# Gated cross-attention with a routed expert layer: pieces of the expert-weight sums stored and fetched at the end of a step, loads behind the turned blocks, and rows of the first pairs fetched ahead of weights

## The chip, the cores and the metric

The kernel runs on one core of a Trainium2 chip. The metric is device time in microseconds (us). One profiled execution is shown beside the timed runs; the names of engines are those of the profile: PE (TensorE matmuls), PEld (its weight loads), DVE (VectorE), ACT (ScalarE), POOL (GpSimd), SP (SyncE, which here only issues DMAs). A name such as L527 is a line of the kernel. A DMA that SP issues is a row marked SPq: its duration is the time that SP spends on issuing it, not the transfer.

## The reference, cut to what matters

There are 32 batches of 112 rows of x and 375 rows of context, 256 wide. All is float32.

```
lat  = layer_norm(layernorm(x));  ctx = layer_norm(ctx_1024)
q    = lat @ Wq                                  # 16 heads of 64
k, v = split(concat([ctx, lat]) @ Wkv)           # 487 keys per batch
x    = x + tanh(g_xattn) * (softmax(q k^T / 8) v) @ Wout
xf   = layernorm(x)                              # 3584 tokens
best two of softmax(xf @ gate_w), renormalised   # 8 experts
y_e  = gelu(xf @ w1[e] + b1[e]) @ w2[e] + b2[e]  # 256 -> 1024 -> 256
out  = x + tanh(g_ffn) * (sum over the two best experts of score * y_e)
```

## The kernel before, in words

**Attention in 128 steps.** A step n (LAST = 128 of them) handles one batch and four of its heads. Eight steps make a group of two batches; m = n mod 8. The keys and values of a pair of batches are made by seven block products instead of eight (`seven`), whose sums run on DVE (L433, L437, L447) and GpSimd (L423). In a step the scores of step n+1 are computed (L483), their maxima are taken on DVE (L493), ACT takes exponentials (L502) and scales them (L516), DVE turns 32x32 blocks in place (`turn_blocks`, L521), and SP sends the turned blocks to memory (`send_blocks`, L527: four DMAs of 256 KB from one of the two buffers `exs`) and takes them back in another layout (`take_blocks`, L534: one DMA of 1 MB into `exT`). `attend` (L547) uses `exT` a step or two later.

**Order.** The program is written with a manual schedule: every engine runs its instructions in the order in which the Python code emits them, SP's DMAs among them. A step is emitted as: turn and send of step n, attend, scores and first exponentials of n+1, and then five slots h = 0 to 4. A slot runs PE units (`slots[h] + pe[h]`), at h = 1 also `take_blocks(n)`, then scalings, and then the small parts listed in `dve[h]` (which run on DVE, ACT, GpSimd or SP). The last slot has PE units alone.

**Other DMAs on SP in a step.** Every fourth step (n mod 4 = 0) up to n = 111 loads a later batch (`load`: 487 KB in three DMAs). At m = 6 and 7 a slab of x is loaded (`load_slab`, L573), and at m = 1 and 2 a finished slab is stored (`residual`, L597). All of these but the store are emitted between send and take.

**Pieces.** The expert layer too uses seven products on 256-row pairs, so sums of blocks of w1 and w2 are needed. They are made during attention in 64 pieces, one a step, from n = 44 to n = 107, and stored in memory (`ws`). `piece_in` (L1272 or L1277) fetches 256 KB in two DMAs into the only buffer `piece`; `piece_sums` are four GpSimd additions in place (L1303), two in each of two slots (h = 2 and 3); `piece_out` (L1314 or L1317) stores four DMAs of 64 KB. At the start of step n, behind the send, the piece of the step before is stored and the next one is fetched into the same buffer; then comes the take.

**Experts.** Tokens are scattered by GpSimd to their experts' places in memory (`xg`, L726) as groups of slabs are routed. 256-row pairs are fetched from `xg` (`fetch_rows`, L935). Pair 0 runs during the last steps with plain weights (`weights_ahead`, `turn_rows(0)`, `hidden_plain`, `second_plain`), from LAST-6 on. In step LAST-2 `others` closes the pools of the attention and opens those of the experts, and fetches the weights of pair 1 for its first layer (`fetch_first`, L988, seven blocks) and second layer (`fetch_second`, L1005, six blocks) and the rows of pairs 1 to 3. After the last step come `second_plain`, the last `attend`, and then the loop over pairs. `turn_rows` transposes rows on PE (L1023) and copies them out of PSUM (L1027).

Of the kernel before, what the change touches and what calls it, by code (L numbers as in the profile page):

```python
# [23 lines left out]
def kernel(  # L24
# [20 lines left out]
    nc = tc.nc  # L45
# [23 lines left out]
    AHEAD = 3  # L69
# [20 lines left out]
    def ended(b):  # L90

        return (SB - 1) * (b // SB) + b % SB - 1 if b % SB else None
# [85 lines left out]
    if True:  # L178
# [344 lines left out]
        def send_blocks(n):  # L523


            for a in range(QB):
                nc.sync.dma_start(  # L527
                    turned[n % 2][:, :, a, :].rearrange("k j n -> j k n"),
                    exs[n % 2][a * QW : (a + 1) * QW].rearrange("j k q c h r -> j k (q c h r)"),
                )  # L530
# [397 lines left out]
        def fetch_rows(t):  # L928
            m, i = unit_of(t)
            r = number(m, i, 1, PADS - 2 * P if t < PAIRS else PADS)  # L930
            pool, n = (found["early"], 1) if t == 0 else (found["rows"], AHEAD + 3)
            xs[t] = pool.tile([P, 2, C], F32, tag="xs", name=f"xs_{t}", bufs=n)
            if t < PAIRS:
                rows_ = xg[bass.ds(r, 2 * P), :].rearrange("(b p) c -> p b c", p=P)
                nc.sync.dma_start(xs[t], rows_)  # L935
            else:
                nc.sync.dma_start(xs[t][:, 0, :], xg[bass.ds(r, P), :])
# [29 lines left out]
        def fetch_first(t):  # L967

            e, new = found["e", t] = expert_of(t)
            fetch_biases(t, e, found["weights"], 2, (0,))  # L970
            if t < PAIRS:
                s1_, s2_, s3_, s4_ = (
                    (f"s{n + 1}", ws1[bass.ds(e, 1), n].rearrange("o p f -> p (o f)"))
                    for n in range(4)
                )
                a11, a12, a22 = (
                    (n, half_of_w1(e, k, h)) for n, k, h in (("11", 0, 0), ("12", 1, 0), ("22", 1, 1))
                )
                order_ = (a11, s2_, s3_, s1_, a22, a12, s4_)
            else:  # L980
                if t == PAIRS:
                    new_weights("21", [P, 512], "s3")
                order_ = [
                    (n, half_of_w1(e, k, h))
                    for n, k, h in (("11", 0, 0), ("12", 1, 0), ("21", 0, 1), ("22", 1, 1))
                ]
            for n, src in order_:
                nc.sync.dma_start(wt[n], src, **new)  # L988

        def fetch_second(t):  # L990

            e, new = found.pop(("e", t))
            if t < PAIRS:
                t1_, t2_, t3_, t4_ = (
                    (f"t{n + 1}", ws2[bass.ds(e, 1), n].rearrange("o p c d -> p (o c) d"))
                    for n in range(4)
                )
                b11, b2x = ("b11", half_of_w2(e, 0, 0, P)), ("b2x", half_of_w2(e, 1, 0, D))
                order_ = (b11, b2x, t4_, t1_, t3_, t2_)
            else:  # L1000
                if t == PAIRS:
                    new_weights("b1x", [P, NF // 2, D], "t12")
                order_ = (("b1x", half_of_w2(e, 0, 0, D)), ("b2x", half_of_w2(e, 1, 0, D)))
            for n, src in order_:
                nc.sync.dma_start(wt[n], src, **new)  # L1005
            fetch_biases(t, e, found["weights"], 2, (1,))
# [236 lines left out]
        def others(ends):  # L1243

            ends.close()
            found["weights"] = ctx.enter_context(tc.tile_pool(name="wexp2", bufs=1))
            found["rows"] = ctx.enter_context(tc.tile_pool(name="rows2", bufs=1))
            found["tiles"] = ctx.enter_context(tc.tile_pool(name="tiles", bufs=2))
            for n in ("11", "12", "22", "s1", "s2", "s3", "s4"):
                new_weights(n, [P, 512])  # L1250
            for n in ("b11", "t3", "t4"):
                new_weights(n, [P, NF // 2, P])
            new_weights("b2x", [P, NF // 2, D])
            new_weights("t12", [P, 2, NF // 2, P])
            wt["t1"], wt["t2"] = wt["t12"][:, 0], wt["t12"][:, 1]
            fetch_first(1)
            fetch_second(1)
            for t in range(1, 1 + AHEAD):
                fetch_rows(t)


        pieces = [(l, e, c) for e in range(E) for l in range(2) for c in range(NF // 2)]
# [166 lines left out]
        for n in range(LAST):  # L1429
            turn_blocks(n, 1)  # L1430
            send_blocks(n)
            if n % NG == 0:
                b = n // NG
                if b + 4 < B:
                    load(b + 4)
                if b == 1:
                    fill()
            g, m = divmod(n, 2 * NG)


# [53 lines left out]
                        dve[h].append(ln_now[h])  # L1494

            k = n - 44
            if 0 <= k <= len(pieces):
                if k > 0:
                    piece_out(k - 1)
                if k < len(pieces):  # L1500
                    piece_in(k)
                    for h, part in enumerate(piece_sums(k)):
                        dve[2 + h].append(part)
            if n == 1:
                nc.scalar.activation(tg[:, :2], tg[:, :2], AF.Tanh)
                nc.scalar.mul(tg[:, 2:3], tg[:, 1:2], 0.5)
# [3 lines left out]
            for u in range(2):  # L1510
                i = ended(2 * g - 2 + u) if g > 0 else None
                if m == 6 + u and ended(2 * g + u) is not None:
                    load_slab(ended(2 * g + u))
                if i is None:
                    continue
                if m == 1:
                    pe[2 + 2 * u].append(lambda i=i: project(i))
                if m == 1 + u:
                    dve[3 - 3 * u].append(lambda i=i: residual(i))

                m_ = 3 + 2 * u if nb >= B else 3 + 3 * u
                if m == m_:
                    dve[0].append(lambda i=i: normed(i))
                    pe[3].append(lambda i=i: gate_turn(i))
                if m == m_ + 1:
                    pe[0].append(lambda i=i: gate_scores(i))
                    if group[i][1] == groups[group[i][0]] - 1:

                        r, (hits, ids, ids_out) = route_parts(group[i][0], nc.gpsimd)
                        extra = [[part] for part in r[:9]] + [[]] + [[part] for part in r[9:11]]  # L1530
                        if group[i][0] == 0:

                            at = [(j, e) for j in range(2) for e in range(0, E, 2)]
                            for k in range(len(at) + 1):
                                extra.append([lambda p=p: ids(*p) for p in at[k - 1 : k] if k > 0])
                                extra[-1] += [lambda p=p: hits(*p) for p in at[k : k + 1]]
                            extra.append([ids_out])
                        extra += [[part] for part in r[11:]]
# [8 lines left out]
            if n == LAST - 6:  # L1547
                soon.close()
                found["early"] = ctx.enter_context(tc.tile_pool(name="early", bufs=1, side="right"))
                weights_ahead()  # L1550
            if n == LAST - 5:
                fetch_rows(0)
            if n == LAST - 3:
                pe[4].append(lambda: turn_rows(0))
            if n == LAST - 2:

                pe[0].append(lambda: others(ends))
                for h in range(1, 5):
                    pe[h].append(lambda h=h: hidden_plain(h - 1, h))
            if n == LAST - 1:  # L1560
                for h in range(4):
                    pe[h].append(lambda h=h: hidden_plain(h + 4, h + 5))
                pe[4].append(lambda: turn_rows(1))
# [7 lines left out]
            for h in range(5):  # L1571
                for unit in slots[h] + pe[h]:
                    unit()
                if h == 4:
                    break
                if h == 1:
                    take_blocks(n)
                if more and h in (1, 3):
                    norm(n + 1, h // 2)
                if more and h == 3:  # L1580
                    turn_blocks(n + 1, 0)
                then_ = soon_[:]
                del soon_[:]
                do(then_)
                for part in dve[h]:
                    part()

                if outgoing and (h % 2 == 0 or n > LAST - NG):
                    outgoing.pop(0)()
                if extra:  # L1590
                    do(extra.pop(0))
                if more and h == 0:
                    exps(n + 1, 1)
# [120 lines left out]
```

## Time and profile before

| what | value |
|---|---|
| median of 3 runs | 2096.77 us (2092.31 to 2097.70) |
| profiled execution | 2101.99 us |
| its span, first to last instruction | 2100.2 us |
| mean granted PE clock | 0.977 |
| PE busy | 1972.9 us (94%) |
| POOL busy | 991.4 us (47%) |
| DMA queue of SP (q1) | 414 MB, 65.0% of 16 engines' span |
| steps with pieces, 44 to 107 | 557.9 to 1373.3 us |

How to read it: a group row of the page gives line, engine, operation, output and input, shapes and count, then busy time and the mean of one in ns, and then idle time of the engine before it and what ended that. A row of a timeline gives start, duration, engine, line, what it writes and reads and how many were merged, and in brackets the idle time before it with what ended it. A row of waits gives who waited for whom, us in total, times, and the longest. A row of a stretch gives its bounds and length, busy time of the engines, granted clock, DMA share and GB/s.

### The profile page before, as it was taken

Reading aid. Unit: us, or ns where it says so; the run is one execution under the profiler, and the core shown is the slowest. Engines: PE = TensorE matmul, PEld = TensorE weight load, DVE = VectorE, ACT = ScalarE, POOL = GpSimd, SP = SyncE. Lnnn points to the kernel's source line nnn. Section 1 sums busy time; section 2 is a strip of 40 time slices with the busy share of each in tenths; the row PEclk is TensorE's granted clock in tenths of the full one; section 3 lists DMA queues with packets and bytes.
Section 4 is the critical chain, followed back from the end, with each engine's and each line's share of the span. In section 5 each row is a group of like instructions: output and inputs, shape, how many; then the busy total and the mean of one; then the engine's idle time right before and its main releaser. Section 6 shows DMA issues by size and latency. Waiting matters only on the chain. (4 is left out here: it accounts for less than half of the span.)

```text
span 2100.2 us, 41466 instructions
## 1 busy us (share of the span) xinstructions
PE 1972.9 (94%) x14352; PEld 1509.7 (72%) x14352; DVE 1340.1 (64%) x2418; ACT 1157.2 (55%) x2717; POOL 991.4 (47%) x1467
## 2 busy tenths in 40 slices
PE   8999999999999999999999998999997899799998
PEld 4676767676766666666767666667675799799887
DVE  6777676867676777676766766676764367445211
ACT  5666666666666665666656655666644133334333
POOL 5533343444356455544555545553333367757312
PEclk9999999999999999999999999999997899999999
DMA  7767666767677777776777767785666366599773
GB/s 212 211 201 206 180 189 176 199 171 223 189 221 225 225 239 232 228 225 219 232 221 214 227 210 224 218 247 172 184 201 203 124 190 192 142 324 295 201 204 58
DMA packets 264643, 433.44 MB, mean 206 GB/s; under 512 B 34312, under 2 KB 152656, under 8 KB 248048
## 3 DMA queue, kind: packets, MB, share of 16 engines
q1 hardware_dynamic: 251968, 414.39, 65.0%
q0 software_dynamic: 11328, 15.33, 3.8%
q8 instruction: 115, 1.88, 0.4%
q10 hardware_dynamic: 1136, 1.05, 0.2%
q14 instruction: 96, 0.79, 0.1%
HBM read 301.37 MB, written 172.28 MB: 226 GB/s over the span
## 5 line engine op out<-in xcount | busy, mean ns | idle before, releaser
L502 ACT ACTIVATE ex<-bank,nmx 128x512 f32<-128x512 f32 x512 | 348.3, 689 | 262.9 <-DVE nmx L493 262.9
L516 ACT ACTIVATE ex<-ex,rc 128x512 f32<-128x512 f32 x512 | 342.2, 718 | 252.2 <-DVE rc L513 250.8
L493 DVE TENSOR_REDUCE nmx<-bank 128x2 f32<-128x974 f32 x256 | 286.1, 1157 | 115.0 <-PE bank L483 114.9
L521 DVE STREAM_TRANSPOSE ex<-ex 128x1024 f32<-128x1024 f32 x256 | 314.9, 1230 | 28.0 <-ACT ex L516 25.2
L1303 POOL TENSOR_TENSOR piece<-piece 128x128 f32<-128x128 f32 x256 | 116.6, 456 | 333.6 <-DMA piece<-in_L_ffn_w_dram 320.0
L413 PEld LDWEIGHTS ps_v<-wkv_s,tT 128*128 128x128 f32 x1536 | 191.8, 194 | 94.2 <-DVE kT L447 44.8
L483 PE MATMUL bank<-kT,qTs 64*128 64x487 f32 x1024 | 249.5, 606 | 0.0
L413 PE MATMUL ps_v<-wkv_s,tT 128*128 128x128 f32 x1536 | 204.0, 281 | 23.0 <-DVE kT L447 21.2
L447 DVE TENSOR_TENSOR vv<-ps_v,vv 128x512 f32<-128x512 f32 x192 | 131.6, 686 | 143.1 <-PE ps_v L413 65.8
L547 PE MATMUL ps_o<-exT,vv 128*64 128x112 f32 (+1 forms) x4096 | 213.1, 262 | 0.6 <-DMA exT<-turned 0.6
L547 PEld LDWEIGHTS ps_o<-exT,vv 128*64 128x64 f32 (+1 forms) x4096 | 199.1, 137 | 9.1 <-DMA exT<-turned 0.8
L407 PE MATMUL ps_k<-tT,wkv_s 128*128 128x487 f32 x378 | 183.2, 586 | 22.1 <-DVE vv L447 22.0
L423 POOL TENSOR_TENSOR kT<-tmpk,kT 128x487 f32<-128x487 f32 x63 | 77.0, 1222 | 243.7 <-ACT kT L441 243.7
L413 PEld LDWEIGHTS ps_v<-wkv,kvT 128*128 128x128 f32 x1024 | 129.4, 192 | 72.9 <-issue 65.3
L1073 POOL DMA_INDIRECT out_dram<-y,xs x60 | 93.4, 1557 | 167.5 <-DVE y L1097 96.3
L483 PEld LDWEIGHTS bank<-kT,qTs 64*128 64x128 f32 x1024 | 89.8, 189 | 106.7 <-issue 96.0
L447 DVE TENSOR_TENSOR kT<-ps_k,kT 128x487 f32<-128x487 f32 x189 | 123.6, 657 | 59.9 <-POOL kT L423 29.7
L423 POOL TENSOR_TENSOR vv<-tmpv,vv 128x512 f32<-128x512 f32 x64 | 81.2, 1270 | 129.9 <-ACT vv L441 129.9
L413 PE MATMUL ps_v<-wkv,kvT 128*128 128x128 f32 x1024 | 141.5, 281 | 0.0
L407 PE MATMUL ps_k<-kvT,wkv 128*128 128x487 f32 x252 | 130.5, 599 | 0.0
L334 PE MATMUL ps_q<-kvT,wq_sb 128*128 128x224 f32 x512 | 120.0, 356 | 1.4 <-ACT kvT L322 0.7
L1119 ACT ACTIVATE h<-h,b 128x256 f32<-128x256 f32 x160 | 66.2, 495 | 97.6 <-DVE h L1128 97.0
(296 smaller groups left out, 3700.6 us busy)
## 6 DMA issues: line engine op xcount, KB each, us to landing
turned<-ex SPq DMA_DIRECT2D x512, 256.0 KB
exT<-turned SPq DMA_DIRECT2D x128, 1024.0 KB
w<-in_L_ffn_w_dram SPq DMA_DIRECT2D x132, 256.0 KB
w_s<-ws SPq DMA_DIRECT2D x80, 256.0 KB
w_t<-ws SPq DMA_DIRECT2D x80, 256.0 KB
w_b2x<-in_L_ffn_w_dram SPq DMA_DIRECT2D x38, 512.0 KB
piece<-in_L_ffn_w_dram SPq DMA_DIRECT2D x128, 128.0 KB
ws<-piece SPq DMA_DIRECT2D x256, 64.0 KB
```

The source lines that it names most:

```text
L334: nc.tensor.matmul(ps, lhsT=wq_sb[:, k, i * P : (i + 1) * P], rhs=kvT[g][:, k, :, SC:NK], start=(k == 0), stop=(k == KD - 1),)
L407: nc.tensor.matmul(ps, lhsT=w[:, 0, i * P : (i + 1) * P], rhs=x[:, :NK], start=True, stop=True)
L413: nc.tensor.matmul(ps[:, c, :], lhsT=x[:, c * P : (c + 1) * P], rhs=w[:, 1, i * P : (i + 1) * P], start=True, stop=True,)
L423: nc.gpsimd.tensor_tensor(v[o], v[l], v[r], ALU.add)
L447: nc.vector.tensor_tensor(v[at], product(n, w, x), v[at], ALU.add)
L483: nc.tensor.matmul(ps[:, j, :NK], lhsT=qT[b // 2, i][r, b % 2].rearrange("p a i -> p (a i)"), rhs=kT[b, i][r, :], start=True, stop=True,)
L493: nc.vector.tensor_reduce(nmx[b, i], pss[b, i][:, :, :NK], AX.X, ALU.max, negate=True)
L502: nc.scalar.activation(exs[n % 2][:, :, p, :, j, :], ps[:, j, :].rearrange("p (c k r) -> p k c r", c=NCK, r=QW), AF.Exp, bias=nmx[b, i][:, ...
L516: nc.scalar.mul(t, t, rc[:, j : j + 1])
L521: nc.vector.transpose(t, t)
L547: nc.tensor.matmul(ps[y * DH : (y + 1) * DH, r, x * S : (x + 1) * S].rearrange("p (a i) -> p a i", a=QB), lhsT=vv[j][:m, c, x, r, y * DH : ...
L1303: nc.gpsimd.tensor_tensor(o, l, r, op) for o, l, r, op in ops
```

## The change

- Loads of batches, the padding of `xg` and the slab loads are collected in a list `after` and emitted behind `take_blocks(n)` instead of in front of it.
- Pieces: a step that sums piece k does so in slots h = 1 and 2; at the end of slot h = 3 it stores piece k and fetches piece k+1. The first piece is fetched at the end of step 43. Both lie behind the take of the step and in front of the send of the next.
- Rows of pair 0 are fetched in step LAST-6 instead of LAST-5, in front of the weights of pair 0, and both behind the take. Their turned copy is made on ACT instead of DVE.
- `others` fetches only the rows of pair 1. The first weights of pair 1 are fetched behind the take of LAST-2; its second weights and the rows of pairs 2 and 3 behind the take of LAST-1.

```diff
@@ others @@
-            fetch_first(1)
-            fetch_second(1)
-            for t in range(1, 1 + AHEAD):
-                fetch_rows(t)
+            fetch_rows(1)
@@ the loop over steps @@
             turn_blocks(n, 1)
             send_blocks(n)
+            after = []
             if n % NG == 0:
                 b = n // NG
                 if b + 4 < B:
-                    load(b + 4)
+                    after.append(lambda b=b: load(b + 4))
                 if b == 1:
-                    fill()
+                    after.append(fill)
...
             k = n - 44
-            if 0 <= k <= len(pieces):
-                if k > 0:
-                    piece_out(k - 1)
-                if k < len(pieces):
-                    piece_in(k)
-                    for h, part in enumerate(piece_sums(k)):
-                        dve[2 + h].append(part)
+            if k == -1:
+                dve[3].append(lambda: piece_in(0))
+            if 0 <= k < len(pieces):
+                for h in range(2):
+                    dve[1 + h].append(lambda k=k, h=h: piece_sums(k)[h]())
+                dve[3].append(lambda k=k: piece_out(k))
+                if k + 1 < len(pieces):
+                    dve[3].append(lambda k=k: piece_in(k + 1))
...
-                    load_slab(ended(2 * g + u))
+                    after.append(lambda i=ended(2 * g + u): load_slab(i))
...
-                weights_ahead()
-            if n == LAST - 5:
-                fetch_rows(0)
+                after += [lambda: fetch_rows(0), weights_ahead]
             if n == LAST - 3:
-                pe[4].append(lambda: turn_rows(0))
+                pe[4].append(lambda: turn_rows(0, nc.scalar.copy))
             if n == LAST - 2:
                 pe[0].append(lambda: others(ends))
+                after.append(lambda: fetch_first(1))
...
             if n == LAST - 1:
+                after += [lambda: fetch_second(1)]
+                after += [lambda t=t: fetch_rows(t) for t in range(2, 1 + AHEAD)]
...
                 if h == 1:
                     take_blocks(n)
+                    do(after)
```

## The prediction, on record before the result

> **What bounds the kernel now.** I read the page first, then busy time by stretch, then the waits of SP's queue in the stretch with pieces, then that queue in order of time, then the end of the attention.
>
> ```profile
> PE 1972.9 (94%) x14352; PEld 1509.7 (72%) x14352; DVE 1340.1 (64%) x2418; ACT 1157.2 (55%) x2717; POOL 991.4 (47%) x1467
> ...
> L1303 POOL TENSOR_TENSOR piece<-piece 128x128 f32<-128x128 f32 x256 | 116.6, 456 | 333.6 <-DMA piece<-in_L_ffn_w_dram 320.0
> ```
>
> TensorE sets the pace nearly everywhere. GpSimd loses 320 us waiting for pieces, which looks like the prize. By stretch (length, then PE, PEld, DVE, ACT and POOL busy, PE clock, DMA share, GB/s), eight steps without pieces, eight with, and all 64 steps with pieces (n = 44 to 107):
>
> ```profile
> 240.40:338.00 97.60, 95.84 (x695) 68.49 (x694) 71.16 (x116) 62.23 (x146) 34.93 (x48) 1.00 0.65 189
> 936.60:1038.00 101.40, 96.50 (x687) 68.31 (x686) 70.21 (x116) 62.21 (x145) 48.27 (x79) 0.97 0.73 229
> 557.90:1373.30 815.40, 768.53 (x5509) 548.68 (x5508) 567.42 (x968) 498.12 (x1154) 435.27 (x728) 0.98 0.73 224
> ```
>
> Eight steps take 97.6 us with PE 98% busy (94.2 where only one slab is projected), so 64 would take about 774. With pieces they take 815. **At most 41 us** can be won from the pieces. What is left on SP there:
>
> ```profile
> SPq L527 <- DVE ex L521: 93.9, 46, 7.4
> SPq L1277 <- DMA ws<-piece: 65.4, 38, 3.5
> SPq L1272 <- DMA ws<-piece: 63.6, 39, 3.5
> ```
>
> SP has only 93.9/64 = 1.5 us a step to spare before the sends (L527), and waits 129 us for piece stores to land. So SP's chain of one step is nearly as long as a step. That chain decides the change, and I cost it from three places: a step without pieces (252), one that is sent right behind exT (1023), one on a free queue (1037).
>
> ```profile
> 252.01 2.71 SPq L527 DMA_DIRECT2D turned<-ex  x4
> 257.99 0.34 SPq L534 DMA_DIRECT2D exT<-turned  x1
> ```
>
> ```profile
> 1022.66 0.36 SPq L534 DMA_DIRECT2D exT<-turned  x1
> 1023.44 2.36 SPq L527 DMA_DIRECT2D turned<-ex  x4
> 1025.89 4.32 SPq L1317 DMA_DIRECT2D ws<-piece  x4
> 1033.84 0.82 SPq L1277 DMA_DIRECT2D piece<-in_L_ffn_w_dram  x2
> ...
> 1037.93 2.61 SPq L527 DMA_DIRECT2D turned<-ex  x4
> 1040.64 3.40 SPq L1317 DMA_DIRECT2D ws<-piece  x4
> 1045.42 0.81 SPq L1277 DMA_DIRECT2D piece<-in_L_ffn_w_dram  x2
> ```
>
> From first send to landed blocks (when L534 is let go): 257.99 - 252.01 = 6.0 us. From first send to landed stores (when the fetch is let go): 7.5 us on the free queue, 1.5 behind the blocks; but 10.4 us where exT was issued 0.8 us ahead. So what is issued behind exT waits for exT: this queue works in order.
>
> **The pieces, part by part.** Before, a step's SP order is send n, store k-1, fetch k, take n. The stores go out behind the send and land 1.5 us after the blocks, so the wait for the blocks is hidden under the store, and exT (1 MB) moves while SP waits for DVE. After, it is send n, take n, store k, fetch k+1, send n+1. Two waits that overlapped now stand one behind the other, and exT's transfer comes between.
>
> The chain from one send to the next:
> - send to landed blocks: 6.0 us, and 0.3 since the fetch of 0.9 us earlier still moves in front: 6.3.
> - exT, issued then: the trace's DMA records end its last 8 KB packet 4.4 us after issue in quiet steps, 4.6 with landing. (From the rows: its data hold the queue 2.9 + 0.8 = 3.7 us, plus some 1.2 of start and landing, 4.9. I take the smaller.)
> - the four stores behind it: 1.5. Their issue, 0.45 each, is hidden under exT.
> - the fetch, which needs the same buffer and so waits for the stores: 0.9 with its gap.
>
> Sum **13.3 us** against 12.2 for a mean step without pieces. In one step of four the loads (487 KB), now between take and store, add 1.6, at exT's 1 MB in about 3.4 us. Slab loads (two of eight steps) add 0.4. Eight steps: 8 x 13.3 + 2 x 1.6 + 2 x 0.4 = 110.4 us; 64 steps: 883.
>
> SP's lateness stalls nobody at once. A send's buffer is written again by the exponentials of two steps on; a send at 275.90 had landed at 282.3 and its buffer was wanted at about 287.8, so 5.5 us of lateness are free. It grows by 4 to 5 in each load step and is used up in the first three or four steps. Then ACT waits at L502 for the send's transfers, and scores, copies and PSUM behind it on ACT hold PE. Some 8 us of lateness are left over at the end and cost nothing: 883 - 8 = 875, against 815: **+60 us**. GpSimd doesn't help: a piece lands about 2 us after a send, its four sums take 4 x 0.456 = 1.8 us, and they are done before the stores' turn comes at 6.6; its 320 us of waiting don't vanish. Bounds of a chain: 12.5 us if exT and stores overlap by engine skew (64 steps 824, +9) and 14.0 if the sums come late behind GpSimd's scatters or exT is stretched (920, +105).
>
> Here a rule speaks for the change. The Trainium skill (DMA: Bandwidth & Descriptors, Anatomy of one DMA) has one DMA at about 2.0 us plus bytes over 436 GB/s, fitted on the GpSimd path. By it, as an estimate, a 1 MB send lands in 4.4, exT in 4.4, the stores 0.6 later, and with the fetch the chain is 10.4 us, shorter than a step: SP would never bind, and the 41 us could be won. The rows show 6.0 for the send, and exT no shorter than the rule's; the rows decide.
>
> The moved loads, slab loads and padding outside these 64 steps: SP has room there (the send waits for DVE in every step), so nothing, at most 1 us either way.
>
> **The end of the attention.** Two stalls there come from order on the DMA queue.
>
> ```profile
> 1561.50 0.41 SPq L935 DMA_DIRECT2D xs<-xg  x1
> ```
>
> ```profile
> 1569.96 1.08 POOL L726 DMA_INDIRECT xg<-xr,sloti  x1 [8.42 <-DMA xs<-xg]
> ...
> 1628.47 1.09 PE L1023 MATMUL ps_x<-ident,xs 128*128 128x128 f32 x4 [8.32 <-DMA xs<-xg]
> ```
>
> First: rows of pair 0 are fetched at 1561.5 behind 2 MB of weights and land at 1569.9; the scatter into xg waits 8.4 us, GpSimd's sums of kT behind it are late, DVE waits 8.9 and PE 4.7, with the clock at half from 1575 to 1585. After, the rows follow exT of step LAST-6: issue near 1554.9, landed near 1559.6. The first scatter (1554.2 before) now waits 5 us, hidden: GpSimd's next sums start at 1557.7 and have 3 us to spare on DVE. The third scatter, which the kT sums follow, comes 5.3 us earlier. The 2 MB now stand before the blocks of step LAST-5 (landed about 1572, 3 us later), hidden as ACT wants their buffer only after DVE's transposes, near 1574. **-7** with the clock (-4 to -10).
>
> Second: PE stands still from 1620.2 to 1628.5 for the rows of pair 1, queued behind 14 transfers. After, they land near 1615. But then attend waits for exT of the last step: its send, held by nine transfers of first weights instead of seventeen of all, goes near 1619, its data behind 1.8 MB land near 1628.5, exT near 1633.2; before, 1639.7. So 8.3 us of wait become 4 of another: **-6** (-3 to -9). The second weights come about 10 us later, near 1640, and are first used after 1670. The copy of pair 0's turned rows on ACT (L1027) comes behind ACT's last scaling (1605.4) instead of two transposes on DVE: -0.4 at most, counted as 0.
>
> **Sum.** The profiled execution took 2101.99 us (span 2100.2 and 1.8 around). 2102 + 60 - 7 - 6 = 2149. The median of the runs, 2096.8, is 5.2 lower, so about **2144 us**.
>
> **Rivals.**
> - The chain doesn't bind (12.1 us or less): then GpSimd gets its pieces early and most of the 41 us come back. 30 to 41 won, and 13 at the end: about 2050. For it: 815 already includes load steps in which SP was late. Against it: the 10.4 us behind exT. Chance 0.13.
> - It cancels: a chain of 12.6 costs 64 x 12.6 + 32 - 8 - 815 = +15 and the end wins 13: 2099. Chance 0.06, of which 0.05 within 0.3% and 0.01 faster.
> - The end gives nothing back, since the half-clock stretches only move: 2157. Chance 0.15.
> - Worse: late pieces also hold GpSimd's in-order queue, where route sums and kT/vv sums stand behind the piece sums, and DVE waits for them; a chain of 14: +105 - 13, 2189. Chance 0.10.
> - My forecast, 2144: chance 0.56, own range 2122 to 2165.
>
> **How the numbers follow.** About 0.3% (6 us) is what a measurement can tell from no change. Faster 0.14, same 0.05, slower 0.81. The range 2090 to 2188 leaves out the first rival and half of the one at 2189. The sign turns at a chain of 12.6 us with the end's 13 won, 0.7 below mine.
>
> **What would show it.** Right: the stretch of 64 steps is 850 to 890 us long with PE busy near 88%; SP's wait for DVE at the sends is almost gone; waits of ACT L502 or of others for the turned blocks' transfers appear; a fetch starts 12 to 13 us after its send; GpSimd still waits about 5 us a step for pieces; the 8.42 and 8.32 rows are gone, and PE waits some 4 us for exT in the last attend. Wrong: fetches that start 11 us or less after the send, or a stretch shorter than 815.

## The result and the profile after

| | before | after |
|---|---|---|
| median of the runs | 2097.23 us (4 runs, 2092.31 to 2102.64) | 2191.64 us (4 runs, 2188.35 to 2192.27) |
| ratio, 95% interval | | 1.0446 [1.0419, 1.0474] |
| span of the profiled execution | 2100.2 us | 2190.6 us |
| mean granted PE clock | 0.977 | 0.963 |
| PE busy | 1972.9 us (94%) | 2014.1 us (92%) |

The changed kernel is 4.5% slower. The forecast was slower too (2144), but only half as much, and the measured time lies just beyond the upper end of the range (2090 to 2188). I first cut both kernels at the same steps. The rows give bounds and length, then PE, PEld, DVE, ACT and POOL busy, PE clock, DMA share and GB/s. Of before, steps 44 to 108 (the 64 with pieces and the one behind them), the stretch up to step 124, step 124, and the rest:

```profile
557.90:1386.60 828.70, 781.31 (x5623) 557.90 (x5622) 577.56 (x982) 506.56 (x1172) 444.91 (x740) 0.98 0.73 225
1386.60:1568.80 182.20, 179.58 (x1281) 128.37 (x1278) 132.54 (x236) 112.11 (x266) 61.80 (x88) 1.00 0.64 194
1568.80:1592.90 24.10, 17.53 (x139) 13.17 (x138) 9.70 (x15) 5.73 (x13) 11.69 (x11) 0.79 0.51 159
1592.90:2100.20 507.30, 453.19 (x3534) 430.91 (x3532) 210.71 (x481) 179.69 (x451) 249.45 (x258) 0.95 0.68 195
```

And of after, the same steps:

```profile
557.50:1482.00 924.50, 823.23 (x5623) 579.57 (x5622) 588.26 (x983) 496.79 (x1172) 446.33 (x741) 0.94 0.70 201
1482.00:1664.20 182.20, 179.58 (x1280) 128.40 (x1278) 131.90 (x235) 111.65 (x265) 60.74 (x88) 1.00 0.64 197
1664.20:1686.80 22.60, 17.59 (x141) 13.92 (x140) 9.93 (x16) 6.00 (x14) 11.32 (x11) 0.85 0.55 175
1686.80:2190.60 503.80, 452.72 (x3534) 431.79 (x3532) 213.35 (x480) 180.62 (x452) 249.46 (x258) 0.95 0.69 196
```

Everything lost is in the first row: 924.5 - 828.7 = **+95.8 us**. The second row is equal to 0.1 us. The end gives back 1.5 and 3.5, together **5.0 us**. The forecast had +60 (for the 64 steps with pieces alone, where it is 908.7 - 815.4 = +93.3, 557.5 to 1466.2 against 557.9 to 1373.3) and -13. In the first row the same 5623 matmuls take 41.9 us more of PE busy time, at a granted clock of 0.94 where it was 0.98, and PE is idle 53.9 us more (101.3 against 47.4): where PE waits more, its clock is lower too.

Who waits now, first in the page of after:

```profile
PE 2014.1 (92%) x14352; PEld 1532.9 (70%) x14352; DVE 1353.0 (62%) x2417; ACT 1148.4 (52%) x2718; POOL 991.4 (45%) x1467
...
L502 ACT ACTIVATE ex<-bank,nmx 128x512 f32<-128x512 f32 x512 | 349.1, 691 | 400.1 <-DMA turned<-ex 220.7
...
L1300 POOL TENSOR_TENSOR piece<-piece 128x128 f32<-128x128 f32 x256 | 116.5, 455 | 420.4 <-DMA piece<-in_L_ffn_w_dram 407.0
```

ACT's exponentials wait 220.7 us for the transfers of the turned blocks; in the same row of before they waited for DVE's maxima alone (262.9). GpSimd's wait for pieces has not shrunk, it grew from 320 to 407. The waits of SP's queue in the stretch with pieces (who waits for whom, us in all, times, longest):

```profile
SPq L534 <- DMA turned<-ex: 206.5, 115, 4.2
SPq L1274 <- DMA ws<-piece: 123.8, 49, 5.0
SPq L1269 <- DMA ws<-piece: 117.8, 51, 4.8
SPq L527 <- DVE ex L521: 10.0, 12, 6.1
```

SP's wait for DVE at the sends, 93.9 us before, is down to 10.0. SP now spends 206.5 + 123.8 + 117.8 = 448 us waiting for its own transfers, in two waits a step. Two steps of SP's queue of after in order of time show them (start, duration):

```profile
764.05 3.10 SPq L527 DMA_DIRECT2D turned<-ex  x4
767.20 0.68 SPq L597 DMA_DIRECT2D out_dram<-x  x1
770.57 0.34 SPq L534 DMA_DIRECT2D exT<-turned  x1
771.02 2.32 SPq L1314 DMA_DIRECT2D ws<-piece  x4
776.90 0.82 SPq L1274 DMA_DIRECT2D piece<-in_L_ffn_w_dram  x2
777.81 2.82 SPq L527 DMA_DIRECT2D turned<-ex  x4
783.88 0.34 SPq L534 DMA_DIRECT2D exT<-turned  x1
784.32 2.01 SPq L1314 DMA_DIRECT2D ws<-piece  x4
789.94 1.74 SPq L1269 DMA_DIRECT2D piece<-in_L_ffn_w_dram  x2
791.72 2.94 SPq L527 DMA_DIRECT2D turned<-ex  x4
```

From the send at 777.81 it is 6.07 us to the take, from the take 6.06 us to the fetch, and 1.78 us to the next send: 13.9 us, all of it issuing or waiting for landings. ACT, in after, a little later:

```profile
797.89 0.69 ACT L502 ACTIVATE ex<-bank,nmx 128x512 f32<-128x512 f32 x1 [5.54 <-DMA turned<-ex]
...
813.13 0.69 ACT L502 ACTIVATE ex<-bank,nmx 128x512 f32<-128x512 f32 x1 [7.33 <-DMA turned<-ex]
```

The exponentials of a step may be written only once an earlier send has left their buffer, so SP's chain reaches ACT, and through the scores PE.

### The profile page after: what moved, and what is told of

Same layout as the page of the kernel before. It is cut to its first block, busy times and chain, and to the rows that moved or that the text cites. A ratio compares the mean times of both kernels' runs of the same rounds, so it can differ in the third digit from the quotient of the medians.

```text
span 2190.6 us, 41518 instructions
## 1 busy us (share of the span) xinstructions
PE 2014.1 (92%) x14352; PEld 1532.9 (70%) x14352; DVE 1353.0 (62%) x2417; ACT 1148.4 (52%) x2718; POOL 991.4 (45%) x1467
## 3 DMA queue, kind: packets, MB, share of 16 engines
q10 hardware_dynamic: 1136, 1.05, 0.2%
## 5 line engine op out<-in xcount | busy, mean ns | idle before, releaser
L502 ACT ACTIVATE ex<-bank,nmx 128x512 f32<-128x512 f32 x512 | 349.1, 691 | 400.1 <-DMA turned<-ex 220.7
L413 PEld LDWEIGHTS ps_v<-wkv_s,tT 128*128 128x128 f32 x1536 | 206.1, 206 | 97.9 <-DVE kT L447 46.1
L483 PE MATMUL bank<-kT,qTs 64*128 64x487 f32 x1024 | 243.8, 594 | 0.0
L413 PE MATMUL ps_v<-wkv_s,tT 128*128 128x128 f32 x1536 | 216.4, 293 | 21.6 <-DVE kT L447 18.2
L547 PEld LDWEIGHTS ps_o<-exT,vv 128*64 128x64 f32 (+1 forms) x4096 | 199.4, 137 | 19.5 <-DMA exT<-turned 9.8
L447 DVE TENSOR_TENSOR kT<-ps_k,kT 128x487 f32<-128x487 f32 x189 | 123.8, 657 | 72.9 <-POOL kT L423 40.2
```

Of the source, the lines that this page charges most:

```text
L413: nc.tensor.matmul(ps[:, c, :], lhsT=x[:, c * P : (c + 1) * P], rhs=w[:, 1, i * P : (i + 1) * P], start=True, stop=True,)
L447: nc.vector.tensor_tensor(v[at], product(n, w, x), v[at], ALU.add)
L483: nc.tensor.matmul(ps[:, j, :NK], lhsT=qT[b // 2, i][r, b % 2].rearrange("p a i -> p (a i)"), rhs=kT[b, i][r, :], start=True, stop=True,)
L502: nc.scalar.activation(exs[n % 2][:, :, p, :, j, :], ps[:, j, :].rearrange("p (c k r) -> p k c r", c=NCK, r=QW), AF.Exp, bias=nmx[b, i][:, ...
L547: nc.tensor.matmul(ps[y * DH : (y + 1) * DH, r, x * S : (x + 1) * S].rearrange("p (a i) -> p a i", a=QB), lhsT=vv[j][:m, c, x, r, y * DH : ...
```

## The experiments

Ratios are to the kernel before on the same chip, whose median was 2097.1 to 2099.1 us. Stretch means steps 44 to 108 as above; diffs are against the changed kernel unless said. A chain is the time from one send to the next in steps 44 to 106, read from SP's queue. The changed kernel's, in means: 13.81 us in 19 plain steps, 13.98 in 14 with a slab load, 14.25 in 14 with a slab store, 15.62 in 16 with loads of a batch, and 14.40 over all. In the kernel before it is 12.74 over all.

### Which part costs: the pieces alone, and all but the pieces

The kernel before with the pieces' new order and nothing else of the change:

```diff
             k = n - 44
-            if 0 <= k <= len(pieces):
-                if k > 0:
-                    piece_out(k - 1)
-                if k < len(pieces):
-                    piece_in(k)
-                    for h, part in enumerate(piece_sums(k)):
-                        dve[2 + h].append(part)
+            if k == -1:
+                dve[3].append(lambda: piece_in(0))
+            if 0 <= k < len(pieces):
+                for h in range(2):
+                    dve[1 + h].append(lambda k=k, h=h: piece_sums(k)[h]())
+                dve[3].append(lambda k=k: piece_out(k))
+                if k + 1 < len(pieces):
+                    dve[3].append(lambda k=k: piece_in(k + 1))
```

> The kernel before with the pieces alone moved (sums in slots 1 and 2, store and fetch at the end of slot 3); loads and slab loads stay in front of the take, and the end of the attention is as before. Theory, SP's chain: send, landed blocks, exT, stores, fetch, next send, one behind the other, set the step. The changed kernel's chain measures 13.8 us plain and 15.6 in load steps; with the loads issued while SP waits for the blocks, a load step should be near 14.1, so 16 x 1.5 = 24 us less than the 96 lost: about 2168 us, at least 2150. Rival, the moved loads or the end of the attention cost the time: near 2097.

Measured: 2196.50 us, ratio 1.046 [1.0424, 1.0497]; stretch 921.7. The pieces' order alone makes the whole loss. The smaller expectation, that loads in front of the take would hide under the send, was wrong: the loss is as large as with the loads behind the take.

The converse has the pieces as before and the rest of the change:

```diff
-            if k == -1:
-                dve[3].append(lambda: piece_in(0))
-            if 0 <= k < len(pieces):
-                ...
+            if 0 <= k <= len(pieces):
+                if k > 0:
+                    piece_out(k - 1)
+                if k < len(pieces):
+                    piece_in(k)
+                    for h, part in enumerate(piece_sums(k)):
+                        dve[2 + h].append(part)
```

> The changed kernel with the pieces put back where they were (stored and fetched at the start of a step, in front of loads and take); loads behind the take and the end of the attention stay changed. SP's chain: the loss is gone and only the gain at the end of the attention is left, 5 us by the trace: 2088 to 2096 us. Rival, the loads behind the take: above 2130.

Measured: 2077.48 us, ratio 0.9895 [0.9877, 0.9913]; stretch 812.3. The rest of the change is worth 1%, more than expected: of the 24.3 us between the spans 16.4 come from the stretch (828.7 - 812.3), which I had at nothing, and 7.6 from the end (step 124 takes 20.0 us, the rest 503.8). In the old order the batch loads stood in front of the stores. With them behind the take, the stores of a load step start 2.81 us after the send instead of 6.06, and the fetch at 8.13 instead of 10.22 (medians of 16). So the loads had stood in the chain of the kernel before.

### Where the loads are issued in the new order

```diff
                 if h == 1:
+                    if n < LAST - 6:
+                        do(after)
                     take_blocks(n)
-                    do(after)
+                    if n >= LAST - 6:
+                        do(after)
```

> The changed kernel with loads and slab loads in front of the take again (all but those of the last six steps). SP's chain: their issue is hidden under the wait for the blocks, some of their transfer too; load steps fall from 15.6 to about 14.2 and slab steps from 14.0 to 13.8: 16 x 1.4 + 14 x 0.2 = 25 us less, about 2167. Rival, GpSimd is held: no change, 2192.

Measured: 2192.82 us, ratio 1.0443 [1.0426, 1.0461]; stretch 922.2: no difference from the changed kernel, and not the 25 us expected. The stores of a load step are issued earlier (6.84 us after the send instead of 8.02), but the fetch starts at 14.50 instead of 14.48. As I read it, the loads' bytes pass between send and stores in any case, on one side of the take or on the other, and the next thing that SP waits for is the landing of those stores. Only where something else hides that landing, as in the order of before, does the place of the loads count.

### Is it the fetch waiting for the stores: two buffers

The second buffer's room comes from one `xin` tile and one `lat` tile; pieces alternate between two pools.

```diff
-            ... tag="xin", name=f"xin_{b}", bufs=4)
+            ... tag="xin", name=f"xin_{b}", bufs=3)
...
-                ... tag="lat", name=f"lat_{b}", bufs=2)
+                ... tag="lat", name=f"lat_{b}", bufs=1)
...
-            v = found["piece"] = rt.tile(...)
+            pool = (rt, io)[n % 2]
+            v = found["piece", n] = pool.tile(...)
```

> The changed kernel with two buffers for the pieces, so that a fetch need not wait for the stores to land; the order of SP's queue is untouched (to make room, three buffers instead of four for x rows and one instead of two for normed rows). SP's chain: without that wait it is 6.1 to the take, 0.4 + 1.9 + 1.1 of issue, about 9.8 us, 11.6 in load steps, below a step of 12.2; steps fall to PE's pace: 2050 to 2085 us. Rival, GpSimd is held by pieces that land behind exT: the fetch still stands behind exT and the stores on the queue, so most of the loss stays, above 2150.

Measured: 2054.36 us, ratio 0.9786 [0.977, 0.9802]; stretch 788.0. SP's queue of this kernel, one step:

```profile
768.92 2.88 SPq L527 DMA_DIRECT2D turned<-ex  x4
775.05 0.34 SPq L534 DMA_DIRECT2D exT<-turned  x1
775.50 1.99 SPq L1312 DMA_DIRECT2D ws<-piece  x4
777.53 0.95 SPq L1270 DMA_DIRECT2D piece<-in_L_ffn_w_dram  x2
778.52 3.45 SPq L527 DMA_DIRECT2D turned<-ex  x4
```

The order of the instructions is that of the changed kernel, but the fetch now follows the stores at once, 2.5 us after the take instead of 6.06 in the rows of after, and the chain falls from 14.40 to 12.14 on average (plain steps 11.12). Stretch 924.5 to 788.0: the one wait for the stores was worth 136 us, more than the loss.

### Is one buffer enough: stores inside the wait for the blocks

All four sums go to slot 0, the stores in front of the take of the same step, the fetch right behind the take. One buffer. (A loop variable `k` elsewhere in the step, which would have hidden this one, is renamed.)

```diff
-                    dve[1 + h].append(lambda k=k, h=h: piece_sums(k)[h]())
-                dve[3].append(lambda k=k: piece_out(k))
+                    dve[0].append(lambda k=k, h=h: piece_sums(k)[h]())
                 if k + 1 < len(pieces):
-                    dve[3].append(lambda k=k: piece_in(k + 1))
+                    after.insert(0, lambda k=k: piece_in(k + 1))
...
                 if h == 1:
+                    if 0 <= k < len(pieces):
+                        piece_out(k)
                     take_blocks(n)
```

> The changed kernel with one buffer, where all four sums are in slot 0, the stores go out in front of the take of the same step, and the fetch right behind the take. If the loss comes from two waits that stand one behind the other, with exT between, then this order hides both: the stores (about 2 us) go out while SP would wait for the blocks, and have landed about 1.5 us after them. Chain: 6.5 to the take, fetch at 8, next send at 9.5: 2050 to 2070 us. Rival, one buffer is what costs: then above 2150.

Measured: 2063.56 us, ratio 0.9845 [0.9815, 0.9874]; stretch 795.4. A step of its SP queue:

```profile
767.52 3.37 SPq L527 DMA_DIRECT2D turned<-ex  x4
773.09 1.79 SPq L1311 DMA_DIRECT2D ws<-piece  x4
775.30 0.33 SPq L534 DMA_DIRECT2D exT<-turned  x1
776.17 0.90 SPq L1269 DMA_DIRECT2D piece<-in_L_ffn_w_dram  x2
779.84 2.71 SPq L527 DMA_DIRECT2D turned<-ex  x4
```

The fetch starts 0.9 us behind the take. The stores stand in front of exT, not behind its 1 MB, and land inside the wait that the send needs anyway. So neither the single buffer nor fetching late is what costs; it is two landings waited for one after the other, with 1 MB between.

### The same bytes on another queue

```diff
-                nc.sync.dma_start(ws1[...], v[:, k, h, :])
+                nc.gpsimd.dma_start(ws1[...], v[:, k, h, :])
...
-                nc.sync.dma_start(ws2[...], v[:, h, j, :])
+                nc.gpsimd.dma_start(ws2[...], v[:, h, j, :])
```

> The changed kernel with the piece stores issued by GpSimd on its own queue, at the same place in the order. SP's chain, if the stores stand behind exT because they are on the same queue: on another queue they needn't, and SP neither issues them nor waits behind them before the fetch for long: fetch at 8.5 to 10 after the send, next send at 11, 2060 to 2100 us; GpSimd pays four issues of about 1 us a step. Rival, exT's transfer holds the engines whatever the queue: fetch still near 12.5, above 2150.

Measured: 2089.30 us, ratio 0.995 [0.9935, 0.9965]; stretch 824.4. In plain steps the fetch starts 8.31 us after the send instead of 12.53, in load steps still 14.47 (medians), and the plain chain fell to 11.4 on average. But the steps are of two kinds. Here are GpSimd's stores of two steps in a row, and then SP's take and fetch of the same two:

```profile
746.74 2.24 POOL L1314 DMA_DIRECT2D ws<-piece  x4
...
759.60 2.21 POOL L1314 DMA_DIRECT2D ws<-piece  x4
```

```profile
750.28 0.34 SPq L534 DMA_DIRECT2D exT<-turned  x1
751.33 0.81 SPq L1274 DMA_DIRECT2D piece<-in_L_ffn_w_dram  x2
...
760.46 0.34 SPq L534 DMA_DIRECT2D exT<-turned  x1
766.28 0.91 SPq L1269 DMA_DIRECT2D piece<-in_L_ffn_w_dram  x2
```

In the first, GpSimd had issued all four stores before the take, and the fetch goes 1.05 us after it. In the second, GpSimd was still issuing until 1.35 us after the take, and the fetch goes 5.82 us after it. So it is in all 47 steps without loads of a batch: in the 22 where the stores were out at most 0.4 us after the take, the fetch follows the take by 1.3 us in the median; in the 25 where they came later, by 5.9 us (5.3 at least), nearly the 6.4 of the changed kernel in the same kind of step. So stores on the other queue escape the wait behind exT only where they are issued ahead of it; issued behind it, they wait about as long as on SP's queue, and the rival of the expectation holds for those steps. The other queue helped because GpSimd can issue before SP takes. The issuing also costs GpSimd about 0.55 us each: it is busy 1134.7 us instead of 991.4, for 256 DMAs.

### Does every microsecond of the chain count

Each piece is stored a second time, to a place that nobody reads, by four more DMAs behind the first four. The new instructions are two lines:

```diff
+            for k in range(4):
+                nc.sync.dma_start(scrap[k], v[:, k // 2, k % 2, :])
```

In the changed kernel:

> The changed kernel with every piece stored twice, the second time to a scratch place that nobody reads (four more stores of 64 KB a step, right behind the first four). If SP's chain sets every one of the 63 steps, what is added to it comes through in full: the four more stores end about 1.5 us later behind exT (their issue, 1.9, lies under exT), 64 x 1.5 = 96 us: 2275 to 2300. If something else has taken over (PE at half clock, GpSimd), less than 50 us come through.

In the kernel with the stores inside the wait:

> The same second set of stores in the kernel with stores in front of the take, where the chain was 10.5 us in the median and SP waited for DVE. SP's chain: 1.9 us more of issue make 12.4, about a step, so only load steps should run over: 2065 to 2100 us, at most a third of what the same stores cost in the changed order.

Measured: 2275.99 us, ratio 1.085 [1.0801, 1.0899], and 2110.43 us, ratio 1.006 [1.0037, 1.0082]. A step of the changed kernel with the second stores:

```profile
765.00 3.76 SPq L528 DMA_DIRECT2D turned<-ex  x4
772.02 0.34 SPq L535 DMA_DIRECT2D exT<-turned  x1
772.47 2.09 SPq L1315 DMA_DIRECT2D ws<-piece  x4
774.60 3.39 SPq L1317 DMA_DIRECT2D scrap<-piece  x4
779.42 0.81 SPq L1275 DMA_DIRECT2D piece<-in_L_ffn_w_dram  x2
780.75 2.94 SPq L528 DMA_DIRECT2D turned<-ex  x4
```

In the changed kernel the addition comes through: +84 us, 1.3 us a step, near the 1.5 that four stores were costed at. Where the stores lie inside the wait, +47 us came through, 56% and not the third at most that I expected. SP's wait for DVE at the sends fell there from 114.4 to 41.1 us in the stretch, so SP still had room, and ACT's exponentials wait 2.2 us for turned blocks, against 276.1 in the changed order with the second stores. The waits point to another path: GpSimd's sums wait 136 us for transfers on SP's queue where it was 34, and PE waits 40.0 us for work that GpSimd does in order with them (`xr` 27.9, `had` 12.1) where it was 5.1. That this path carries the 47 us was not tested.

### Weights in flight beside the scatters at the end

Here only the fetch of pair 0's weights moves, from LAST-6 to LAST-5:

```diff
-                after += [lambda: fetch_rows(0), weights_ahead]
+                after += [lambda: fetch_rows(0)]
+            if n == LAST - 5:
+                after += [weights_ahead]
```

> The changed kernel with the 2 MB of weights of pair 0 fetched a step later (behind the take of LAST-5 instead of LAST-6). In the changed kernel the first scatter of the last group took about 7 us to let the next one go, where it was 3.6 before. If the weights in flight stretch it, the second scatter follows the first by about 5 us instead of 7.3, the kT sums behind the third come 3 us earlier and step LAST-4 shrinks from 22.6 to about 19.5 us, 3 us in all. Rival, the scatters land slowly anyway: step LAST-4 stays at 22 to 23.

Measured, in a single execution: 2189.59 us; step 124 takes 25.4 us, where 19.5 was expected and the changed kernel takes 22.6. GpSimd's queue there, in the changed kernel (in brackets the idle time before and what ended it):

```profile
1656.56 1.14 POOL L726 DMA_INDIRECT xg<-xr,sloti  x1 [7.66 <-DVE nmx L493]
...
1663.84 1.08 POOL L726 DMA_INDIRECT xg<-xr,sloti  x1 [2.25 <-DMA xg<-xr,sloti]
...
1667.55 0.98 POOL L726 DMA_INDIRECT xg<-xr,sloti  x1 [2.21 <-DMA xg<-xr,sloti]
1668.54 1.23 POOL L423 TENSOR_TENSOR kT<-tmpk,kT 128x487 f32<-128x487 f32 x1
```

and with the weights a step later:

```profile
1654.27 1.14 POOL L726 DMA_INDIRECT xg<-xr,sloti  x1 [7.61 <-DVE nmx L493]
...
1659.47 1.08 POOL L726 DMA_INDIRECT xg<-xr,sloti  x1 [0.17 <-issue]
...
1668.15 0.98 POOL L726 DMA_INDIRECT xg<-xr,sloti  x1 [7.19 <-DMA xg<-xr,sloti]
```

In these rows a scatter starts only when the one before has landed. In the changed kernel the first pair is 7.3 us apart and the second 3.7. With the weights moved it is 5.2, of which the last part is GpSimd's own work (the row waits 0.17 us), and 8.7. The long gap went where the 2 MB went: in the nine traces with the new end and the weights in LAST-6 the first pair is 6.5 to 7.3 us apart and the second 2.9 to 4.8, and only here is it the other way round. But 2 MB are not needed for a long gap: in the kernel before, the scatters at 881.6, 1163.3 and 1372.8 us, far from these weights, also came 7.3 to 7.5 us after the one ahead, released by its landing. The kernel did not get faster, because the third scatter is the one that the kT sums stand behind.

### The best version found

The order of the kernel before with two buffers, and the rest of the change: the diff of the pieces put back, plus that of the two buffers.

> Pieces in the order of before (store and fetch between send and take) with two buffers, and the rest of the change kept (loads behind the take, end of the attention). SP's chain without the wait for landed stores: 2.7 + 3.3 + 0.9 and a take that finds its blocks landed, about 7.5 us, under the shortest step of 9: the pieces cost no more than their share of DMA, 64 steps near 785 us: 2040 to 2060 us. Rival, the transfers themselves fill the queue: not below the 2054 of two buffers in the changed order.

Measured: 2043.61 us, ratio 0.9744 [0.9714, 0.9773], about 6.8% below the changed kernel. Its stretch, and SP's largest wait in it:

```profile
557.30:1333.20 775.90, 762.30 (x5625) 549.00 (x5624) 581.74 (x983) 505.27 (x1172) 447.97 (x740) 1.00 0.80 241
```

```profile
SPq L527 <- DVE ex L521: 169.5, 56, 7.4
```

PE is busy 98% at full clock, and SP waits for DVE again, 169.5/65 = 2.6 us a step. GpSimd's sums still wait some 214 us here for transfers of pieces, against some 34 with the stores inside the wait, which is the slower of the two: GpSimd's waiting, the largest figure on the page of before, was no measure of the time.

## Why the prediction was right in kind and short in size

**The mechanism was right.** It rested on one claim, that SP's chain is nearly as long as a step and that two landings now stand one behind the other. Most of the signs asked for came: SP's wait for DVE nearly gone, ACT L502 waiting for the turned blocks, a fetch 12.5 us after its send in plain steps, PE at 89% in the stretch, GpSimd's wait still there. One did not: the 64 steps took 908.7 us, not 850 to 890. The pieces alone made the loss, and removing the one wait reversed it. The prediction put the wait of the stores down to SP's queue, which "works in order"; GpSimd's stores, issued behind exT on another queue, waited about as long, so the queue is not the reason or not the only one.

The rule that was weighed, the Trainium skill's DMA: Bandwidth & Descriptors, Anatomy of one DMA, gave a chain of 10.4 us as an estimate (its terms add to 10.3). Measured were 13.8 in the plainest steps, so the rows were the right choice.

**The step that failed is the sum of the chain: each term a little short, and one left out.** The prediction had 13.3 us for a plain step and 13.8 over all; measured are 13.81 and 14.40. By kind of step, excess times number:

| steps | forecast | measured mean | excess x number |
|---|---|---|---|
| plain | 13.3 | 13.81 | 0.51 x 19 = 9.7 us |
| slab store | 13.3 | 14.25 | 0.95 x 14 = 13.3 us |
| slab load | 13.7 | 13.98 | 0.28 x 14 = 3.9 us |
| batch load | 14.9 | 15.62 | 0.72 x 16 = 11.5 us |

That sums to 38 us, all of the 36 between +60 and +95.8. The terms of the sum, in means of plain steps:
- Send to landed blocks: 6.34, forecast 6.3.
- exT and the four stores behind it (take to fetch): 6.37, forecast 4.6 + 1.5 = 6.1. In the DMA records exT's last packet now ends 4.94 us after issue (median). I had weighed 4.4 from quiet steps against 4.9 from the queue's rows and taken the smaller one; with other transfers behind it, the larger was right. (The step that I called a free queue was not quite one: its send at 1037.93 has an exT 3.2 us ahead of it, issued at 1034.77.)
- Fetch to next send: 1.10, forecast 0.9.
- The stores of finished slabs (L597), two of eight steps and one DMA more in the queue between send and take or ahead of the send: not counted at all. They cost about 0.45 us beyond a plain step.
- Batch loads: 1.8 us beyond a plain step (15.62 - 13.81), forecast 1.6.

Over the 63 steps exT with its stores makes some 17 of the 38 us, fetch to send 13, and the slab stores 6. None is large in one step. But 64 steps multiply every half microsecond by 64, and the doubled stores show that such an addition reaches the end of the program. Of the 48 us between 2144 and 2191.6, 36 are the chain's, 8 the end's (below), and the rest comes from the 5.2 us taken off for the profiled execution of before, where that of after is only 0.6 above its median.

**The lateness left over at the end** was right: 8 us forecast; in step 108 the send goes 7.4 us after its blocks are turned, and two steps on the delay is 0.8, with no cost in the stretch behind.

**"At most 41 us" was too low.** The best version takes 52.8 us out of the stretch (828.7 - 775.9). The ceiling was scaled from one stretch of eight steps without pieces, in which PE is busy 95.84/8 = 12.0 us a step; in the best version it is 762.3/65 = 11.7, so those eight were dearer than the mean. It decided nothing in the forecast, but as a ceiling it would have undervalued the prize.

**The moved loads** were costed at nothing outside the 64 steps, and that held: step 44 starts at 557.5 against 557.9. Within the new piece order their place does not matter. In the old order it was worth 16 us.

**The end, first stall: -7 forecast, -1.5 measured.** The 8.42 us row is gone, as expected. The step that failed is "the third scatter comes 5.3 us earlier". In step 124 the kT sums behind it start 4.3 us after the step's start (1668.54 - 1664.2), where they started 6.8 after it before: 2.5 us won. The first scatter waits 7.66 us rather than the 5 forecast. Its row names DVE, but the semaphore that it waits for itself is one of SP's DMAs, and it last moved at 1655.76, 5.8 us after the rows' fetch was issued at 1649.97. From the first scatter to the third it then takes 7.29 + 3.71 = 11.0 us, where the forecast left under 10 (from 1559.6 to 1574.65 - 5.3). The 2 MB of weights in flight stretch the first of these gaps: moving them moved it, in one execution. Gaps as long occur without them too, and why a scatter takes longer is open.

**The end, second stall: -6 forecast, -3.5 measured** (507.3 to 503.8, and 508.1 to 503.8 against the pieces alone). The 8.32 us row is gone and PE waits for exT in the last `attend` instead, as forecast, 5.78 us and not 4. exT came in time: the last `attend` starts 40.7 us after the start of step 125 (1727.47 - 1686.8), where it started 46.8 after it before, 6.1 won. What the forecast left out is that the work behind the wait is slower: those 48 matmuls take 4.39 us at a granted clock of 0.56, where before they took 2.53 at 1.00, and so 4.3 us are left when `attend` ends, 3.5 at the end of the program. PE's row of before and that of after:

```profile
1639.75 2.53 PE L547 MATMUL ps_o<-exT,vv 128*64 128x112 f32 x48 [0.58 <-DMA exT<-turned]
```

```profile
1727.47 4.39 PE L547 MATMUL ps_o<-exT,vv 128*64 128x112 f32 x48 [5.78 <-DMA exT<-turned]
```

These splits are of single executions. From step 124 to the end it took 526.4 us in after and 521.3 to 526.9 in the eight other traces with the same new end, against 531.4 in before and 533.4 with the pieces alone moved: the new end wins some 4.5 to 12 us.

**The rivals.** That the chain doesn't bind, and that it cancels, are refuted. "Worse, a chain of 14" gave 2189 and came nearest. Of its two reasons the second, a stretched exT, is part of the truth. The first, late sums, is not: SP's stores wait only some 13 us for GpSimd in the whole stretch. New waits of DVE for route sums on GpSimd do exist (41.3 us in all, 2.7 before), but they can't set the period: in the chain steps above, DVE has the blocks turned 10.7 to 12.8 us before SP sends them. I held the two bounds of the chain 1.5 us apart and then gave the upper one a tenth. Since each of its terms had only been measured in quieter surroundings than the new order makes, more of the chance belonged above 13.3 than below.

## What to carry to other kernels

Before moving a DMA that waits, write out the issuing queue's chain for one period and mark which landings are waited for side by side and which one behind the other; a small store issued behind a megabyte, here even on another queue, costs most of that megabyte's time if anything waits for the store. When the chain is near the period, cost every instruction in it, rare steps too, and take each duration from the busiest row at hand. A wait of an engine that doesn't set the pace is no prize: find the queue that does, and give it a second buffer, or put its short transfers inside a wait that is there anyway.

## What the runs showed of the hardware that was not expected

- Moving three load DMAs across the take on the same queue moved the issue of the stores by 1.2 us, and the fetch that waits for their landing by nothing (14.48 and 14.50 us after the send).
- Four stores that GpSimd issued on its own queue waited behind a megabyte on SP's queue about as long as on SP's own: the fetch that needs them came 5.9 us after the take, 6.4 on SP's queue, and 1.3 where they were issued ahead of it (medians).
- A scatter by GpSimd, released when the one before lands, came 6.5 to 8.7 us after it with 2 MB of weights in flight on SP's queue. Without these weights, in the steps of attention ahead of them, such gaps were 2.9 to 8.4 us over all traces.
- PE's clock was lower where PE waited more. For the same matmuls in the stretch with pieces: in the best version 13.6 us idle, 762.3 busy at a clock of 1.00; before, 47.4 idle, 781.3 busy at 0.98; after, 101.3 idle, 823.2 busy at 0.94; with the doubled stores, 154.9 idle, 854.1 busy at 0.91. The 95.8 us lost are 53.9 of idle PE and 41.9 of longer matmuls.
